# Moving the B multiply of the last state group from VectorE to GpSimd in a selective scan

## The chip, the core and the metric

The kernel runs on one core of a Trainium2 chip. Its five engines work side by side, each through its own instruction queue in order: TensorE (PE in the profile; its weight loads are PEld), VectorE (DVE), ScalarE (ACT), GpSimd (POOL) and SyncE (SP), which here only issues DMAs. The metric is the device time of one execution in microseconds, as the median of repeated runs.

## The reference

Two layers of a Perceiver-like model are applied to `x` of shape (16, 64, 256) in float32. Layer 0 has cross attention to a context of 1601 rows, a selective scan (Mamba) and a spiking feed-forward network. Layer 1 has a windowed cross attention with rotary embedding, a self attention with a distance mask, and a mixture of 8 experts. The change is in the selective scan of layer 0, which works on 512 channels and 16 states:

```python
def _selective_scan(u, delta, a, b, c):
    deltaA = jnp.exp(jnp.einsum('bld,dn->bldn', delta, a))
    deltaBu = jnp.einsum('bld,bln,bld->bldn', delta, b, u)

    def step(h, inp):
        dA_t, dBu_t, c_t = inp
        h = dA_t * h + dBu_t
        y = jnp.einsum('bdn,bn->bd', h, c_t)
        return (h, y)
    ...
    _, ys = lax.scan(step, h0, xs)
```

For each channel and state this is an elementwise product (delta·u times B), a linear recurrence along the 64 tokens of a batch row, a second product (with C), and a sum over the 16 states.

## The kernel before

The 1024 tokens are 8 tiles of 128. For the scan they are gathered in five groups of 1, 2, 2, 2 and 1 tiles (`GROUPS`), so a group has T = 128 or 256 token columns. `l0_ssm_prelude` computes for a group the projections, the convolution, delta and delta·u, and writes delta, delta·u, B and C to DRAM scratch. `l0_ssm_state` reads them back, laid out for the scan: the 128 partitions hold 4 states times 32 channels, and a tile of 4·T columns holds four such blocks of 32 channels. So one pass of the loops below handles one block of 128 channels (`c`, 4 of them) and one group of 4 states (`m`, 4 of them), and there are 5 × 4 × 4 = 80 passes. In each pass:

- ScalarE computes the decays exp(delta·a) with four activations (line 898) into one of two buffers `decay0`, `decay1` (`NDEC = 2`), used in turn;
- VectorE multiplies `rep["du"]` (delta·u) by B into a tile `hs` (line 906). There are two `hs` buffers (`HSB = 2`), so a pass can only start its multiply when the pass two before it has been consumed by TensorE;
- VectorE runs the recurrence in place over `hs` with one scan instruction (line 908);
- VectorE multiplies `hs` by C in place (line 909);
- TensorE adds up the states with four matmuls against `fold` into the PSUM tile `y_ps` (line 912).

B and C come in the tiles `bc0` (state groups 0 and 1) and `bc1` (2 and 3), broadcast over the four blocks of 32 channels. After the four state groups of a channel block, VectorE multiplies `y_ps` by the gate into `yg` (line 917). The tiles `rep_delta` and `rep_du` have two buffers each (`REPB = 2`) and are loaded by DMAs that SP issues (line 882).

GpSimd does smaller elementwise work elsewhere, among it: the softplus sum `spv` of the prelude (line 843, which is followed by the DMA to `d_delta`), the bias `xnb` of the first softmax (lines 605 to 607), the additions of bias rows to `x` (lines 543, 734, 1087, 1202), the rotary products `ku` and `kT` (line 1071) and the head-masked keys `ke` (line 1127) of the second cross attention.

The order of all this is not written out by hand. The program is built in a `TileContext` with `schedule_with_timeline_sim=True`: a list scheduler replays the instructions against a cost table (`scheduler_costs`) and chooses, by priority, what each engine issues next. The priorities are shifted by the table `AT`, with one number for each tile of cross attention (`C`), each group's prelude (`P`) and state part (`S`), each stage of the later layers (`D`) and the setup (`W`). So a change in the cost or the engine of one instruction, or in `AT`, can move any instruction on any queue. `Stream.new` gives out the working tiles of the later layers, with `BBUFS = 3` buffers for the larger ones.

Of the kernel before, what the change touches and what calls it, by code (L numbers as in the profile page):

```python
# [20 lines left out]
P = 128  # L21
B, L, D = 16, 64, 256
# [43 lines left out]
ABUFS, BBUFS, EBUFS = 6, 3, 4  # L66
# [17 lines left out]
WA = (0, 1)  # L84
GLAST = 0
SAFT = 1
AT = {'C': [-2654, 4379, 8514, -4563, 12435, 8604, 5776, 4319], 'P': [2517, -15292, 2786, -8356, -3704], 'S': [-11856, -1695, 3457, 4667, 7019], 'D': [634, 2469, 3629, 3736, 1255, 2078, 12241, 1395, 3496, 7769, 6287, -759, -2896, 7604, 9413, 8837, 2220, -6795, 6561, -231, 6259, 13545, -16171, 16810, 10814, 6655, 15499, 7678, 3528, 7791, 7607, 15099], 'W': [22194, 1512]}
LH = 1
PRI_D = [0] * 8
MOEB = {7:('bank0','bank1')}  # L90
# [8 lines left out]
PB = 8  # L99
PADX, PADR, PADC, SPLD, SPLM = 1, 1, 1, 1, 1  # L100
VPV = 0
ST1 = 1
SILU2 = 1
LNX, LNV, VBA, DSK = 1, ('c', 'p'), 1, 1
# [33 lines left out]
ABUFS = 6  # L138
BBUFS = 3
# [77 lines left out]
def kernel(ctx: ExitStack, tc: tile.TileContext, a: dict, out: bass.AP):  # L217
    nc = tc.nc
    A, V, G = nc.scalar, nc.vector, nc.gpsimd
# [41 lines left out]
    def sized(pool, tag, k, T, bufs=1, most=None):  # L261

        t = pool.tile([P, k * (most or GT)], F32, tag=tag, name=tag, bufs=bufs)
        return t[:, 0 : k * T].rearrange("p (k t) -> p k t", k=k)
# [90 lines left out]
    def at(kind, k):  # L355
        c = tc.cur_priority
        v = AT[kind][k]
        with tc.high_priority(0 if v is None else c - v):
# [4 lines left out]
    def after(k):  # L363
        return nullcontext() if k is None or k not in pe else tc.issue_after(pe[k].ins)

    def layernorm(new, bank, stp, x, nt):

        h = new("h", [P, nt, D])
        hT = new("hT", [P, KC, nt * P])
        mv = stp.tile([P, nt, 2], F32, tag="mv", name="mv")  # L370
        for j in range(nt):
# [50 lines left out]
    def mm_tok(ps, srcT, w, j):  # L422

        nk = w.shape[1]
        for kc in range(nk):
            nc.tensor.matmul(  # L426
                ps, srcT[:, kc, j * P : (j + 1) * P], w[:, kc, :],
                start=(kc == 0), stop=(kc == nk - 1),
            )
# [284 lines left out]
    def l0_ssm_prelude(w, pp, late, banks, g):  # L714
# [96 lines left out]
        for hf in range(2):  # L811
# [30 lines left out]
            V.copy_predicated(lg, mk, du)  # L842
            (V if VPV else G).tensor_add(vp, vp, lg)
            V.tensor_mul(du, vp, ug[:, 2 * hf : 2 * hf + 2, :])
# [17 lines left out]
    def l0_ssm_state(w, pp, s, g):  # L862
        i0, nt = GROUPS[g]
        T, nb = nt * P, 2 * nt
        x = xs[g]
        bc = []
        for q in range(2):
            t = sized(pp, f"bc{q}", 4, T)
            src = s["bc"][q * DST : (q + 1) * DST, :].rearrange("(k n) t -> n k t", n=SN)
            for n in range(SN):  # L870
                nc.sync.dma_start(
                    out=t[n * SD : (n + 1) * SD, :, :], in_=src[n].partition_broadcast(SD)
                )
            bc.append(t)
        yg = sized(pp, "yg", NE, T)
        for c in range(NE):
            rep = {}
            for k in ("delta", "du"):
                t = sized(pp, "rep_" + k, 4, T, bufs=REPB)
                src = s[k][c * P : (c + 1) * P, :].rearrange("(k d) t -> d k t", d=SD)  # L880
                for n in range(SN):
                    nc.sync.dma_start(out=t[n * SD : (n + 1) * SD, :, :], in_=src)
                rep[k] = t
            y_ps = psS.tile([P, T], F32, tag="y", name="y_ps")
            if DSK and SPLD:
                for k in range(4):
                    r = slice(k * SD, (k + 1) * SD)
                    nc.tensor.matmul(
                        y_ps[r, :], w["Dd"][:, c, r], s["ug"][:, c, :], start=True, stop=False
                    )  # L890
            elif DSK:
                nc.tensor.matmul(y_ps, w["Dd"][:, c, :], s["ug"][:, c, :], start=True, stop=False)
            for m in range(NG):
                da = w["decay"][turns[0] % NDEC][:, 0 : 4 * T]
                turns[0] += 1
                dav = da.rearrange("p (b l) -> p b l", l=L)
                for k in range(4):
                    A.activation(  # L898
                        dav[:, k * nb : (k + 1) * nb, 1:],
                        rep["delta"][:, k, :].rearrange("p (b l) -> p b l", l=L)[:, :, 1:],  # L900
                        AF.Exp,
                        scale=w["am"][:, c * 4 + k, m : m + 1],
                    )
                hs = sized(pp, "hs", 4, T, bufs=HSB)
                shp = [P, 4, T]
                V.tensor_mul(hs, rep["du"], bc[m // 2][:, m % 2, :].unsqueeze(1).to_broadcast(shp))  # L906
                hf = hs.rearrange("p k t -> p (k t)")
                V.tensor_tensor_scan(hf, da, hf, 0.0, ALU.mult, ALU.add)  # L908
                V.tensor_mul(hs, hs, bc[m // 2][:, 2 + m % 2, :].unsqueeze(1).to_broadcast(shp))  # L909
                with tc.high_priority(10**6):  # L910
                    for k in range(4):
                        nc.tensor.matmul(  # L912
                            y_ps[k * SD : (k + 1) * SD, :], fold, hs[:, k, :],
                            start=(m == 0 and not DSK), stop=(m == NG - 1),
                        )
            if DSK:
                V.tensor_mul(yg[:, c, :], y_ps, s["ug"][:, NE + c, :])
                continue
            V.scalar_tensor_tensor(
                yg[:, c, :], s["ug"][:, c, :], w["D"][:, c : c + 1], y_ps, ALU.mult, ALU.add  # L920
            )
            G.tensor_mul(yg[:, c, :], yg[:, c, :], s["ug"][:, NE + c, :])
        ps = psS.tile([P, nt, D], F32, tag="y", name="so_ps")
        for j in range(nt):
            mm_tok(ps[:, j, :], yg, w["out_w"], j)
        V.tensor_add(x, x, ps)
# [4 lines left out]
    class Stream:  # L931
# [9 lines left out]
        def new(self, name, shape):  # L941
            big = math.prod(shape[1:]) > D
            return self.pool.tile(
                shape, F32, tag=f"{'b' if big else 'a'}{self.k}", name=name,
                bufs=BBUFS if big else ABUFS,
            )

        def hidden(self):
# [498 lines left out]
    with tc.tile_pool(name="c0", bufs=1, side="right") as wp, tc.tile_pool(  # L1447
# [44 lines left out]
        for g, (i0, nt) in enumerate(GROUPS):  # L1492
            for i in range(i0, i0 + nt):
                hv, hs = HC.get(i, (None, None))
# [26 lines left out]
            if g < STATES:  # L1521
                with at("S", g):
                    l0_ssm_state(ws, sp, scratch[g], g)
# [105 lines left out]
    for i in range(NTI):  # L1629
        if i == RES:  # L1630
            tags = [("rep_delta", REPB), ("rep_du", REPB), ("hs", HSB), ("bc0", 1), ("bc1", 1)]
            tags = [t for t in tags for _ in range(t[1])]
            for e in range(NX):
                tag, bufs = tags[e]
                t = sized(sp, tag, 4, GT, bufs=bufs).rearrange("p (k c) n -> p k c n", k=2)
                for k in range(2):
                    nc.sync.dma_start(
                        out=t[:, k],
                        in_=a[f"L1_ffn_w{k + 1}"][e].rearrange("(c p) n -> p c n", p=P),
                    )  # L1640
                experts[e] = [t[:, 0], t[:, 1]]
        if TILE_STREAM[i] == NSTREAM:
            streams.append(LateStream(sp, NSTREAM, [(psS, t, 1) for t in BANK4]))
            vb, pb = (t[:, 0:n] for t, n in zip(ws["decay"], (2 * D, P)))
            for t in (vb, pb):
                G.memset(t, 0.0)
            if PADR or PADC:
                t = ws["decay"][1][:, P : P + PW]
                G.memset(t, 0.0)
                G.memset(t[:, 2:3], 1.0)  # L1650
                pads.append(t.unsqueeze(1))
            wx["vb"].append(vb.rearrange("p (b j h d) -> p b j h d", b=2, h=2, d=DH))
            wa["pb"].append(pb.unsqueeze(1))
        later(i)
        for g in range(STATES, len(GROUPS)):
            if i == AFTER[g]:
                with at("S", g), tc.issue_after(done[HOLD[g]]) if g in HOLD else nullcontext():
                    l0_ssm_state(ws, sp, scratch[g], g)
# [109 lines left out]
```

## Time and profile before

| quantity | value |
|---|---|
| median of 3 runs | 739.54 us (738.85 to 741.94) |
| profiled execution | 737.56 us |
| its span, first to last instruction | 735.7 us |
| PE busy | 631.6 us (86%) |
| DVE busy | 535.5 us (73%) |
| ACT busy | 453.2 us (62%) |
| POOL busy | 199.2 us (27%) |
| mean granted TensorE clock | 0.925 |

The profiled execution takes 1.9 us more than its span and lies 2.0 us under the median of the runs. Busy shares are averages over stages with different limits. The scan passes run from 87 us (first multiply, line 906) to about 565 us (last product with `fold`, line 912); the groups follow each other with passes of 128x512 for the first group until about 155 us, passes of 128x1024 for the three middle groups from about 158 to 488 us, and passes of 128x512 for the last group after that. Before lies the start of the first cross attention, behind it the rest of the later layers.

### The profile page before, as it was taken

To read this page: it belongs to the slowest core of one execution; us is meant where nothing else is said; L and a number is where in the kernel's file an instruction comes from. 1 tells how busy PE (TensorE), PEld (TensorE's weight loads), DVE (VectorE), ACT (ScalarE), POOL (GpSimd) and SP (SyncE) were. 2 spreads that over 40 slices of the span, in tenths; PEclk is the share of its full clock that TensorE was granted. 3 is DMA by queue.
4 is the path that set the end of the run, shared out by engine and by line. 5 is a ranking of instruction groups with operands and counts; after the bars stand their busy time and mean duration, and the time that the engine had idled before them with its cause. 6 is when DMAs were issued, how large, how long until landed. Compare 5 with 4: busy or idle time off the path is not lost.

```text
span 735.7 us, 12927 instructions
## 1 busy us (share of the span) xinstructions
PE 631.6 (86%) x4508; PEld 446.4 (61%) x4508; DVE 535.5 (73%) x937; ACT 453.2 (62%) x1442; POOL 199.2 (27%) x300
## 2 busy tenths in 40 slices
PE   9989888879997699864878695779889999999997
PEld 7555455535443487631536473357678787789986
DVE  3424578889999889999999899999776334444432
ACT  3446557845686458954987674478475657755422
POOL 3110020110003238033132966611053421133000
PEclk9999999989999679986889998599999999999999
DMA  8999699799834941122043021025457422000000
GB/s 302 333 367 356 185 324 289 257 270 353 256 120 122 318 132 30 37 67 71 1 128 97 2 58 30 11 62 140 143 169 244 122 58 73 9 1 8 8 15 7
DMA packets 85382, 102.55 MB, mean 139 GB/s; under 512 B 11515, under 2 KB 67763, under 8 KB 85190
## 3 DMA queue, kind: packets, MB, share of 16 engines
q1 hardware_dynamic: 85318, 101.74, 44.9%
q8 instruction: 35, 0.57, 0.3%
q14 instruction: 29, 0.24, 0.1%
HBM read 96.33 MB, written 5.37 MB: 138 GB/s over the span
## 4 chain that ended last, share of the span: by engine, by line
PE 47%; DVE 23%; ACT 11%; DMA 8%; POOL 5%; issue 5%; SPq 2%; DVEq 0%; POOLq 0%; ACTq 0%
PE he_ps L416 8%; PE eo_ps L426 7%; DVE hs L908 6%; DVE hs L906 5%; DVE hs L909 4%; PE s_ps L587 4%; PE o_ps L632 4%; ACT decay L898 3%; DMA w<-in_L_ffn_w 2%; PE fc_ps L416 2%; PE in_ps L416 2%; PE s_ps L1132 1%; PE pj_ps L426 1%; PE qk_ps L416 1%; DMA Wv<-in_L_attn_Wv 1%
## 5 line engine op out<-in xcount | busy, mean ns | idle before, releaser
L908 DVE TENSOR_TENSOR_SCAN hs<-decay,hs 128x1024 f32<-128x1024 f32 (+1 forms) x80 | 156.6, 1962 | 1.0 <-ACT decay L898 0.4
L898 ACT ACTIVATE decay<-rep_delta,ssm 128x252 f32<-128x252 f32 (+1 forms) x320 | 121.9, 455 | 50.7 <-DVE hs L908 36.7
L906 DVE TENSOR_TENSOR hs<-rep_du,bc 128x1024 f32<-128x1024 f32 (+1 forms) x80 | 86.9, 1091 | 19.3 <-PE y_ps L912 10.0
L909 DVE TENSOR_TENSOR hs<-hs,bc 128x1024 f32<-128x1024 f32 (+1 forms) x80 | 87.1, 1094 | 0.0
L1429 DVE SCALAR_TENSOR_TENSOR x<-eo_ps,pad,x 128x256 f32<-128x256 f32 x56 | 26.8, 479 | 46.1 <-PE eo_ps L426 45.5
L912 PE MATMUL y_ps<-hs,fold 128*32 128x256 f32 (+1 forms) x640 | 47.7, 383 | 14.5 <-DVE hs L909 14.2
L1418 ACT ACTIVATE he<-he_ps,late 128x128 f32<-128x128 f32 x112 | 35.1, 367 | 39.1 <-PE he_ps L416 39.0
L632 PE MATMUL o_ps<-cn,prT 128*64 128x256 f32 x384 | 52.5, 397 | 2.4 <-ACT prT L629 2.4
L587 PE MATMUL s_ps<-cT,qkT 128*64 128x512 f32 (+1 forms) x256 | 54.2, 509 | 0.2
L1127 POOL TENSOR_TENSOR ke<-kT,hmask 128x512 f32<-128x512 f32 x28 | 41.2, 1491 | 42.1 <-PE s_ps L1132 41.5
L632 PEld LDWEIGHTS o_ps<-cn,prT 128*64 128x64 f32 x384 | 28.1, 141 | 21.0 <-issue 5.9
L416 PE MATMUL in_ps<-hT,L_attn_in_proj_wT 128*128 128x256 f32 (+1 forms) x160 | 35.1, 371 | 4.5 <-ACT ug L760 3.8
L1139 ACT ACTIVATE sm<-s_ps,wmx 128x64 f32<-128x64 f32 x112 | 33.4, 322 | 3.5 <-DVE wmx L1136 3.4
L912 PEld LDWEIGHTS y_ps<-hs,fold 128*32 128x32 f32 x640 | 14.3, 113 | 34.4 <-DVE hs L909 19.8
L416 PEld LDWEIGHTS in_ps<-hT,L_attn_in_proj_wT 128*128 128x128 f32 x160 | 27.6, 210 | 12.5 <-ACT ug L760 5.5
L407 PE MATMUL pt_ps<-ident,h 128*128 128x128 f32 x88 | 20.4, 324 | 16.4 <-ACT h L395 13.6
L416 PE MATMUL he_ps<-hT,w 128*128 128x128 f32 x192 | 27.9, 291 | 7.5 <-DMA w<-in_L_ffn_w 7.1
L416 PE MATMUL fc_ps<-hT,L_ffn_W_fcT 128*128 128x128 f32 x224 | 32.3, 292 | 2.1 <-ACT f L998 1.6
L416 PEld LDWEIGHTS fc_ps<-hT,L_ffn_W_fcT 128*128 128x128 f32 x224 | 29.4, 202 | 7.2 <-ACT f L998 3.3
L765 DVE SCALAR_TENSOR_TENSOR ug<-xpad,ssm,ug 128x256 f32<-128x256 f32 (+1 forms) x60 | 26.4, 461 | 8.9 <-ACT ug L760 8.6
L605 POOL TENSOR_TENSOR xnb<-xmx,qb 128x1 f32<-128x1 f32 x8 | 2.7, 339 | 108.4 <-DVE xmx L594 91.9
L587 PEld LDWEIGHTS s_ps<-cT,qkT 128*64 128x64 f32 x256 | 17.5, 136 | 23.7 <-issue 20.0
(396 smaller groups left out, 1484.8 us busy)
## 6 DMA issues: line engine op xcount, KB each, us to landing
cn<-in_ctx SPq DMA_DIRECT2D x48, 512.0 KB, 5.4
cT<-in_ctxT SPq DMA_DIRECT2D x42, 512.0 KB, 8.2
w<-in_L_ffn_w SPq DMA_DIRECT2D x48, 256.0 KB, 2.7
rep_delta<-d_delta SPq DMA_DIRECT2D x48, 128.0 KB, 2.7
rep_du<-d_du SPq DMA_DIRECT2D x48, 128.0 KB, 3.1
bc<-d_bc SPq DMA_DIRECT2D x24, 128.0 KB, 3.6
rep_delta<-d_delta SPq DMA_DIRECT2D x32, 64.0 KB, 2.2
rep_du<-d_du SPq DMA_DIRECT2D x32, 64.0 KB, 2.1
```

What stands on the lines that cost most here:

```text
L416: last = nc.tensor.matmul(ps, w[:, kc, oc * P : (oc + 1) * P], src[:, kc, :], start=(kc == 0), stop=(kc == nk - 1),)
L426: nc.tensor.matmul(ps, srcT[:, kc, j * P : (j + 1) * P], w[:, kc, :], start=(kc == 0), stop=(kc == nk - 1),)
L587: nc.tensor.matmul(s_ps[r * L : (r + 1) * L, :n], q["qkT"][:, kc, r * L : (r + 1) * L], cT[r][:, kc, :], start=(kc == 0), stop=(kc == KC - 1),
L632: q["last"] = nc.tensor.matmul(q["o"][r * L : (r + 1) * L, :], prT[:n, j % 4, r * L : (r + 1) * L], cn[r, j], start=(j == 0), stop=(j == NKB),
L898: A.activation(dav[:, k * nb : (k + 1) * nb, 1:], rep["delta"][:, k, :].rearrange("p (b l) -> p b l", l=L)[:, :, 1:], AF.Exp, scale=w["am" ...
L906: V.tensor_mul(hs, rep["du"], bc[m // 2][:, m % 2, :].unsqueeze(1).to_broadcast(shp))
L908: V.tensor_tensor_scan(hf, da, hf, 0.0, ALU.mult, ALU.add)
L909: V.tensor_mul(hs, hs, bc[m // 2][:, 2 + m % 2, :].unsqueeze(1).to_broadcast(shp))
L912: nc.tensor.matmul(y_ps[k * SD : (k + 1) * SD, :], fold, hs[:, k, :], start=(m == 0 and not DSK), stop=(m == NG - 1),)
L1127: G.tensor_mul(ke, kT[:, c, tok].unsqueeze(1).to_broadcast([P, HPC, L]), hmask.unsqueeze(2).to_broadcast([P, HPC, L]),)
L1139: A.activation(sm[:, k, :], s_ps[:, k, :], AF.Exp, bias=nmx[:, k : k + 1], accum_out=su[i][:, c * HPC + k : c * HPC + k + 1],)
L1418: A.activation(he[:, oc, :], ps[:, oc, :], AF.Relu, bias=w["b1"][:, e * KC + oc : e * KC + oc + 1],)
```

## The change

For the last state group (`m == 3`) of every channel block, and for all five token groups, the multiply by B is issued to GpSimd in place of VectorE. The switch is a table `PM` from token group to pairs (state group, which multiply); the second multiply can be switched in the same way but no entry does so. A name `SHORT` could shorten a stream's buffers; it is empty, so nothing changes there. The table `AT` has new numbers throughout.

```diff
-AT = {'C': [-2654, 4379, 8514, -4563, 12435, 8604, 5776, 4319], 'P': [2517, -15292, 2786, -8356, -3704], 'S': [-11856, -1695, 3457, 4667, 7019], 'D': [634, 2469, ...], 'W': [22194, 1512]}
+AT = {'C': [-6091, 4373, 9420, -4172, 12134, 6772, 6015, 5883], 'P': [1045, -22019, 3863, -10472, -4579], 'S': [-20080, -1481, 3644, 6320, 7606], 'D': [699, 3387, ...], 'W': [23447, -4680]}
...
+SHORT = ()
+PM = {g: ((3, 0),) for g in range(5)}
...
-                V.tensor_mul(hs, rep["du"], bc[m // 2][:, m % 2, :].unsqueeze(1).to_broadcast(shp))
+                (G if (m, 0) in PM.get(g, ()) else V).tensor_mul(
+                    hs, rep["du"], bc[m // 2][:, m % 2, :].unsqueeze(1).to_broadcast(shp)
+                )
                 hf = hs.rearrange("p k t -> p (k t)")
                 V.tensor_tensor_scan(hf, da, hf, 0.0, ALU.mult, ALU.add)
-                V.tensor_mul(hs, hs, bc[m // 2][:, 2 + m % 2, :].unsqueeze(1).to_broadcast(shp))
+                (G if (m, 1) in PM.get(g, ()) else V).tensor_mul(
+                    hs, hs, bc[m // 2][:, 2 + m % 2, :].unsqueeze(1).to_broadcast(shp)
+                )
...
-                bufs=BBUFS if big else ABUFS,
+                bufs=BBUFS - (self.k in SHORT) if big else ABUFS,
```

So 20 multiplies change their engine, 12 of 128x1024 elements and 8 of 128x512. In the order in which the two programs are built, VectorE has 20 instructions fewer and GpSimd 20 more; on the other engines the instructions are the same and stand in a somewhat different order.

More of the change, by code (lines that the diff above doesn't have):

```diff
@@ L86 @@
 SAFT = 1
-AT = {'C': [-2654, 4379, 8514, -4563, 12435, 8604, 5776, 4319], 'P': [2517, -15292, 2786, -8356, -3704], 'S': [-11856, -1695, 3457, 4667, 7019], 'D': [634, 2469, 3629, 3736, 1255, 2078, 12241, 1395, 3496, 7769, 6287, -759, -2896, 7604, 9413, 8837, 2220, -6795, 6561, -231, 6259, 13545, -16171, 16810, 10814, 6655, 15499, 7678, 3528, 7791, 7607, 15099], 'W': [22194, 1512]}
+AT = {'C': [-6091, 4373, 9420, -4172, 12134, 6772, 6015, 5883], 'P': [1045, -22019, 3863, -10472, -4579], 'S': [-20080, -1481, 3644, 6320, 7606], 'D': [699, 3387, 5747, 3268, 1810, 2473, 14139, 1370, 3464, 7908, 4834, 1211, -4408, 8955, 8776, 12666, 2862, -6570, 6663, 390, 6477, 11509, -19814, 15316, 10812, 10825, 15642, 6273, 4889, 7190, 7666, 14068], 'W': [23447, -4680]}
 LH = 1
```

## The prediction

> **What bounds the kernel now.** I read the table of stretches first (busy time of each engine in chosen stretches), because busy shares over the whole span mix stages with different limits. Columns: PE, PEld, DVE, ACT and POOL busy microseconds, granted clock, DMA share, GB/s.
>
> ```profile
> 85.00:165.00 80.00, 64.36 (x493) 38.38 (x492) 65.77 (x111) 54.45 (x139) 10.91 (x14) 0.94 0.91 272
> 165.00:490.00 325.00, 255.49 (x1719) 161.87 (x1718) 310.90 (x407) 216.12 (x646) 123.07 (x124) 0.86 0.36 107
> ...
> 500.00:565.00 65.00, 59.25 (x528) 48.21 (x526) 49.91 (x90) 40.36 (x148) 12.86 (x20) 0.95 0.58 170
> 565.00:735.70 170.70, 163.85 (x1199) 140.08 (x1199) 69.07 (x215) 93.28 (x369) 36.12 (x84) 0.99 0.14 41
> ```
>
> From 165 to 490 us, where the three groups of two tiles are scanned, DVE is busy 310.90 of 325 us (96%) and PE 79%: DVE sets the pace there. Before (first group) DVE is at 82%, after 500 us PE at 91% and then 96%. So a microsecond of DVE time counts nearly in full in the middle stretch, partly at its edges. The second view is the groups of instructions by line and shape (busy us, mean ns of one, idle before them).
>
> ```profile
> L908 DVE TENSOR_TENSOR_SCAN hs<-decay,hs 128x1024 f32<-128x1024 f32 x48 | 115.7, 2411 | 0.4
> L906 DVE TENSOR_TENSOR hs<-rep_du,bc 128x1024 f32<-128x1024 f32 x48 | 64.9, 1354 | 7.9 <-DMA rep_du<-d_du 5.6 <-PE y_ps L912 2.3
> ...
> L906 DVE TENSOR_TENSOR hs<-rep_du,bc 128x512 f32<-128x512 f32 x32 | 22.0, 696 | 11.4 <-PE y_ps L912 7.7 <-DMA rep_du<-d_du 3.2 <-DMA cT<-in_ctxT 0.5
> ```
> ```profile
> L843 POOL TENSOR_TENSOR spv<-spv,hT 128x512 f32<-128x512 f32 x6 | 9.6, 1605 | 52.2 <-DVE hT L842 33.8 <-ACT spe L826 9.8 <-ACT decay L898 8.6
> ...
> L1127 POOL TENSOR_TENSOR ug<-ug,hmask 128x512 f32<-128x512 f32 x4 | 4.1, 1042 | 0.3 <-PE s_ps L1132 0.3
> ...
> L1071 POOL TENSOR_TENSOR ug<-ug,late 128x256 f32<-128x256 f32 x2 | 1.3, 639 | 0.0
> ```
>
> The reader should see two things. The mean of L906 at 128x1024 is 1354 ns, but most of its instructions take 1.21 us; and POOL's L843 has a mean of 1605 ns, while its shortest takes 1264. Something lengthens both. The third view, the timeline, shows what (start us, us):
>
> ```profile
> 170.88 1.27 POOL L734 TENSOR_TENSOR x<-x,L_attn_out_proj_b 128x512 f32<-128x512 f32 x1 [15.19 <-DVE h L385]
> ```
> ```profile
> 170.95 2.28 DVE L906 TENSOR_TENSOR hs<-rep_du,bc 128x1024 f32<-128x1024 f32 x1
> 173.27 2.29 DVE L908 TENSOR_TENSOR_SCAN hs<-decay,hs 128x1024 f32<-128x1024 f32 x1
> ```
> ```profile
> 328.00 5.05 POOL L734 TENSOR_TENSOR x<-x,L_attn_out_proj_b 128x256 f32<-128x256 f32 x1 [1.60 <-DVE h L385]
> ```
>
> POOL's addition runs from 170.88 to 172.15. The DVE multiply that starts at 170.95 takes 2.28 us: the 1.20 us until POOL is done, and then 1.08, its usual time. The other way round, POOL's 128x256 addition at 328.00, which takes 0.73 us undisturbed, takes 5.05 while DVE issues a multiply, a scan and other instructions with two SBUF inputs back to back. So DVE and POOL do not overlap in such work; they take turns.
>
> **What is removed.** Twelve DVE multiplies of 128x1024 and eight of 128x512. Start to start they cost 1.135 and 0.60 us (medians over the undisturbed ones of L906; the recorded 1.21 and 0.68 overlap the next instruction by 0.08). Sum: 12 × 1.135 + 8 × 0.60 = 18.4 us of DVE.
>
> **What is added.** The same multiplies on POOL, which the trace does not show there. The nearest rows are its multiplies with one operand broadcast over an outer dimension: L1071 (0.64 us for 256 columns) and L1127 (1.04 for 512), both from a stretch where DVE leaves POOL alone. The line through them gives 1.85 us for 1024. The additions without a broadcast give 0.72 and 1.265, so 2.35 for 1024; that is the upper bound. POOL's queue gets 12 × 1.85 + 8 × 1.04 = 30.5 us (upper bound 12 × 2.35 + 8 × 1.265 = 38.3), beside 123 of 325 us in the middle stretch: it does not become the bound by its amount.
>
> **What DVE pays for it.** If the two took no notice of each other, DVE would be 18.4 us shorter. The trace says otherwise. The eight 128x512 additions of L843 and L734 that fall between 138 and 330 us lengthened the DVE instructions under them by 1.09, 0.44, 1.10, 1.04, 1.00, 0.99, 0.79 and 0.78 us, in mean 0.90 of their own 1.265: all but 0.36 us. L1127's twenty in the same kind of stretch cost DVE 0.59 of 1.04: all but 0.45. I take 0.40 us off each: the time in which POOL starts up, or DVE happens to run something that reads PSUM or one tile. Then a moved multiply of 1024 costs DVE 1.45 and saves 1.135, net +0.32 us; one of 512 costs 0.64 and saves 0.60, net +0.04. Sum: 12 × 0.32 + 8 × 0.04 = +4.1 us. The bounds: every POOL microsecond stalls DVE, 30.5 − 18.4 = +12.1; or the average of the whole stretch from 160 to 500 us holds, where all DVE lengthenings together are 30.5 us for 63.4 us of undisturbed POOL reading work, a share of 0.48, which gives 14.6 − 18.4 = −3.8. That average counts many 128x1 instructions that hardly read, so I stay with the rows of the large ones.
>
> The Trainium skill has a rule that speaks against this change (SBUF — State Buffer, "Who interferes with whom"): a DVE instruction with two SBUF inputs and a GpSimd instruction that reads SBUF shut each other out, and whichever began first keeps the shared port for its whole length. Taken to the letter, with DVE always second, the sum would be the +12.1 already given; the rows above say somewhat less.
>
> **The new wait.** The scan of `m == 3` (L908) now waits for POOL. What is queued behind it on DVE is its own multiply by C, the next block's multiplies and whatever the later layers have there, and ACT waits too, since the decay buffers come free with the scans (ACT idled 36.7 us on L908 before). In the built order DVE has the scan and the C multiply of `m == 2` ahead of it, 2.20 + 1.135 us, and other work: the stretch has 310.9 − 48 × 4.47 = 96 us of it, 2.0 us a pass; 5.3 us together, counted from the C multiply of `m == 1`, which frees the `hs` buffer. POOL needs the four L912 matmuls (4 × 0.44 = 1.8), its 1.85, and the wait for its turn: all POOL instructions together took 0.85 times longer than undisturbed there, so about 1.6. That is 5.2: just covered, so zero; without that cover it costs up to 1.6 us a block, 12 × 1.6 = 19.
>
> **What else moves.** On POOL the moved multiply stands ahead of `xnb` (L605, ACT's first softmax waits for it), `spv` (L843, then SP's `d_delta` DMA; SP's queue waited 21.5 us for it before) and the `ke` pairs (PE). POOL stood idle 91.9 us before L605 and 41.5 before L1127, waiting for others, so 2 to 3 us of delay lie beside DVE's work: zero. `rep_du`'s loads on SP (L882, which waited 16.9 us for L906) now wait for POOL's read; with two buffers they have a whole block of time: zero. The new `AT` table moves instructions on every queue, but ahead of the last scan DVE has the same other work to within 1% and the same 80 passes in the same order: zero, with bounds of ±3 us from the largest single DVE waits in the stretch (2.7 us, L906 for a DMA). `SHORT` is empty: zero.
>
> **Sum.** The profiled execution is 735.7 of span + 1.9 around it = 737.6 us; +4.1 gives 741.7. Its time lies 2.0 under the median of the runs, 739.54, so the forecast is 743.6 us.
>
> **The rivals.** One half percent, 3.7 us, is about what a measurement here can tell from no change.
>
> *Gain by overlap (faster).* POOL's multiplies fall where DVE reads PSUM or waits, as in the stretch from 400 to 500 us, where the share of POOL time that DVE paid was 0.31: 9.5 − 18.4 = −8.9; with the share 0.48, −3.8. So 730.6 to 735.7. It decides if the share is under 0.60 − 3.7/30.5 = 0.48. For it speaks that DVE no longer holds its queue at L906 for `y_ps` (7.7 us in the 512 rows). Against it: scans and `hs` multiplies of 128x1024, all with two SBUF inputs, are 115.7 + 64.9 + 63.5 = 244 of DVE's 311 us there.
>
> *Break-even.* The share is between 0.48 and 0.72 and nothing waits: within 3.7 us of 739.5.
>
> *Slower by the turn-taking.* My forecast, share 0.72 and more, up to 1: +4 to +12, 743.6 to 751.6.
>
> *Slower by the wait at the scan.* POOL gets its turn late, as at 328.00, in half the blocks: 6 × 1.6 = 10 on top of break-even, 749; it decides once POOL's waits exceed the cover of 5.3 us.
>
> **How the numbers follow.** Turn-taking 0.36, wait at the scan 0.11, break-even 0.18, overlap 0.35. So faster 0.35, same 0.18, slower 0.47. The range goes from the lower overlap case, 730.6, to just above the full turn-taking, 753. The forecast's own range is 740 to 752.
>
> **What would show it.** Right: in the changed kernel L908 and the C multiplies that start just after a POOL multiply are longer by about 1.4 us, POOL's multiplies take 1.85 us undisturbed and more in the mean, and the middle stretch is longer with DVE still above 95% busy. Wrong: DVE lengthenings that grow by less than 15 us in total, or scans of `m == 3` with long idle time before them released by POOL, or a stretch other than 165 to 490 that changes.

## The result: 2.8% slower, and the profile after

The changed kernel takes 759.34 us (median of 4 runs, 757.79 to 759.61); the kernel before takes 739.19 us on the same chip (4 runs). The ratio is 1.0277, 95% interval 1.0218 to 1.0337. The forecast was 743.6 with a range of 730 to 753, so the sign of the likeliest case was right and the size was not: +20.2 us where +4.1 was forecast. The profiled spans differ by as much, 756.1 against 735.7. Of the runs of the variants below, two executions that were slow as a whole are left out of the medians: one of `a_mid` (829.91 us, at a granted clock of 0.72 where its others have 0.91 to 0.92) and one of `a_memset_q` (760.41 us).

First the page's busy times, then the table of stretches of the changed kernel, cut where its groups begin and end. Columns: PE, PEld, DVE, ACT and POOL busy microseconds with instruction counts, granted clock, DMA share, GB/s. Code lines have moved in the changed kernel: the multiply by B is L908, the scan L912, the multiply by C L913, the fold L918.

```profile
PE 635.5 (84%) x4508; PEld 450.5 (60%) x4508; DVE 538.9 (71%) x917; ACT 450.6 (60%) x1442; POOL 248.2 (33%) x320
```
```profile
85.00:165.00 80.00, 64.34 (x483) 37.43 (x480) 65.15 (x106) 52.86 (x135) 18.10 (x18) 0.94 0.90 275
165.00:525.00 360.00, 277.67 (x1860) 181.65 (x1859) 324.97 (x420) 229.31 (x713) 157.78 (x138) 0.84 0.34 99
525.00:590.00 65.00, 56.58 (x513) 44.85 (x511) 54.24 (x101) 39.62 (x142) 25.61 (x38) 0.97 0.60 175
590.00:756.10 166.10, 158.51 (x1149) 136.21 (x1141) 63.74 (x199) 89.06 (x350) 31.67 (x69) 1.00 0.13 39
```

DVE has 20 instructions fewer (917 against 937) and is busy 3.4 us longer. The middle stretch has become longer, 360 us against 325, and DVE is busy 90% of it against 96%: it has both more busy time and more idle time. The groups by line and shape show where the busy time comes from (busy us, mean ns of one, idle before), first DVE's, then POOL's:

```profile
L913 DVE TENSOR_TENSOR hs<-hs,bc 128x1024 f32<-128x1024 f32 x48 | 66.2, 1381 | 0.1
L908 DVE TENSOR_TENSOR hs<-rep_du,bc 128x1024 f32<-128x1024 f32 x36 | 49.6, 1380 | 10.3 <-PE y_ps L918 4.5 <-DMA rep_du<-d_du 3.2 <-DMA bc<-d_bc 2.6
```
```profile
L908 POOL TENSOR_TENSOR hs<-rep_du,bc 128x1024 f32<-128x1024 f32 x12 | 32.9, 2738 | 52.9 <-PE y_ps L918 23.0 <-DMA rep_delta<-d_delta 16.5 <-DMA cn<-in_ctx 13.4
...
L908 POOL TENSOR_TENSOR hs<-rep_du,bc 128x512 f32<-128x512 f32 x8 | 12.0, 1505 | 43.3 <-PE y_ps L918 43.1
```

DVE's 36 multiplies by B at 1024 columns take 1380 ns in the mean, where the undisturbed ones take 1.21 us; POOL's take 2738, where its undisturbed ones take 2.35 us. Each lengthens the other. The timeline shows single moved multiplies with the DVE instruction that meets them (start us, us):

```profile
223.30 2.86 POOL L908 TENSOR_TENSOR hs<-rep_du,bc 128x1024 f32<-128x1024 f32 x1 [17.12 <-PE y_ps L918]
224.53 1.91 DVE L833 TENSOR_SCALAR spm<-spe 128x512 uint8<-128x512 f32 x1 [0.29 <-ACT spe L828]
...
346.58 2.47 POOL L908 TENSOR_TENSOR hs<-rep_du,bc 128x1024 f32<-128x1024 f32 x1 [16.50 <-DMA rep_delta<-d_delta]
346.77 4.43 DVE L912 TENSOR_TENSOR_SCAN hs<-decay,hs 128x1024 f32<-128x1024 f32 x1
...
375.94 2.35 POOL L908 TENSOR_TENSOR hs<-rep_du,bc 128x1024 f32<-128x1024 f32 x1 [3.02 <-PE y_ps L918]
376.10 2.50 DVE L844 COPY_PREDICATED hT<-spm,h 128x256 f32<-128x256 uint8 x1
```

The scan at 346.77 takes 4.43 us where 2.2 is usual; the small instruction at 376.10, whose shortest takes 0.46, takes 2.50 and ends just after POOL does. These two began inside a POOL multiply and stood until it was done. It isn't only instructions with two input tiles that stand: the comparison L833 (`tensor_scalar`, one input tile, 128x512) that starts at 224.53 inside the multiply of 223.30 takes 1.91 us, where three others of its shape take 0.39 to 0.40. The undisturbed multiply takes POOL 2.35 us at 1024 columns and 1.27 at 512.

To see the whole of it I split DVE's time from its first instruction to the last scan into three parts, from the trace: gaps between instructions (idle); what each instruction takes over the tenth percentile of its own operation, tile and shape (lengthening); and the rest (plain). The same split is used for the experiments. The last four columns come from one profiled execution each; those of `b_shrunk` and `a_shrunk` lie 3 to 4 us under their medians, so differences of that size in the time of the last scan say nothing.

| kernel | median us (before, same chip) | idle | lengthening | plain | last scan at |
|---|---|---|---|---|---|
| before | 739.19 | 95.9 | 41.4 | 421.5 | 560.5 |
| after | 759.34 (739.19) | 112.9 | 63.1 | 406.9 | 584.6 |
| `b_shrunk` | 736.85 (738.24) | 108.2 | 40.5 | 406.2 | 556.5 |
| `a_shrunk` | 736.97 (738.24) | 111.7 | 39.4 | 407.0 | 559.7 |
| `b_plus` | 750.73 (739.78) | 94.5 | 41.5 | 437.8 | 575.4 |
| `b_all` | 713.92 (739.78) | 137.2 | 37.2 | 359.6 | 535.5 |
| `q_zero` | 743.63 (738.70) | 129.0 | 33.5 | 414.5 | 578.7 |
| `q_fill` | 746.39 (738.70) | 129.8 | 34.3 | 415.0 | 580.9 |
| `q_mul` | 762.92 (738.70) | 119.8 | 58.7 | 414.8 | 595.2 |
| `a_edge` | 737.78 (738.00) | 107.5 | 45.3 | 406.6 | 561.3 |
| `a_mid` | 759.40 (738.00) | 114.6 | 59.7 | 406.7 | 583.0 |

From before to after, plain time falls by 14.6 (the 18.4 removed, less other work that now lies ahead of the last scan, about 2.5 us of it by the shortest times of these instructions), lengthening rises by 21.7, and idle time rises by 17.0: the last scan is 24.1 later, and the tail behind it 3.7 shorter. The added idle time is hardly a wait for POOL: with POOL's multiplies cut (`a_shrunk`) it is 111.7, nearly the same.

### The profile page after: what moved, and what is told of

It is laid out like the page before. It is cut to its first block, busy times and chain, and to the rows that moved or that the text cites. A ratio compares the mean times of both kernels' runs of the same rounds, so it can differ in the third digit from the quotient of the medians.

```text
span 756.1 us, 12976 instructions
## 1 busy us (share of the span) xinstructions
PE 635.5 (84%) x4508; PEld 450.5 (60%) x4508; DVE 538.9 (71%) x917; ACT 450.6 (60%) x1442; POOL 248.2 (33%) x320
## 4 chain that ended last, share of the span: by engine, by line
PE 29%; DVE 6%; DMA 5%; POOL 4%; issue 3%; ACT 2%; SPq 1%; POOLq 0%; DVEq 0%
PE he_ps L418 7%; PE eo_ps L428 7%; DMA w<-in_L_ffn_w 4%; DVE hs L912 2%; PE s_ps L1138 2%; PE pj_ps L428 2%; PE fc_ps L418 1%; PE o_ps L1166 1%; DVE hs L913 1%; POOL hs L908 1%; PE pt_ps L409 1%; DVE hs L908 1%; PE f_ps L1353 1%; POOL ke L1133 1%; PE p_ps L1155 1%
## 5 line engine op out<-in xcount | busy, mean ns | idle before, releaser
L912 DVE TENSOR_TENSOR_SCAN hs<-decay,hs 128x1024 f32<-128x1024 f32 (+1 forms) x80 | 157.4, 1973 | 5.7 <-POOL hs L908 5.4
L913 DVE TENSOR_TENSOR hs<-hs,bc 128x1024 f32<-128x1024 f32 (+1 forms) x80 | 90.0, 1130 | 0.1
L908 DVE TENSOR_TENSOR hs<-rep_du,bc 128x1024 f32<-128x1024 f32 (+1 forms) x60 | 66.2, 1107 | 17.4 <-PE y_ps L918 8.3
L908 POOL TENSOR_TENSOR hs<-rep_du,bc 128x1024 f32<-128x1024 f32 (+1 forms) x20 | 44.9, 2245 | 96.2 <-PE y_ps L918 66.0
L918 PE MATMUL y_ps<-hs,fold 128*32 128x256 f32 (+1 forms) x640 | 49.0, 388 | 30.3 <-DVE hs L913 30.3
L918 PEld LDWEIGHTS y_ps<-hs,fold 128*32 128x32 f32 x640 | 14.3, 114 | 50.0 <-DVE hs L913 38.2
L428 PE MATMUL pj_ps<-L_ffn_W_projT,f 128*128 128x256 f32 x112 | 32.1, 439 | 1.6 <-ACT f L1005 0.9
```

The source lines that it names most:

```text
L428: nc.tensor.matmul(ps, srcT[:, kc, j * P : (j + 1) * P], w[:, kc, :], start=(kc == 0), stop=(kc == nk - 1),)
L908: (G if (m, 0) in PM.get(g, ()) else V).tensor_mul(hs, rep["du"], bc[m // 2][:, m % 2, :].unsqueeze(1).to_broadcast(shp))
L913: (G if (m, 1) in PM.get(g, ()) else V).tensor_mul(hs, hs, bc[m // 2][:, 2 + m % 2, :].unsqueeze(1).to_broadcast(shp))
L918: nc.tensor.matmul(y_ps[k * SD : (k + 1) * SD, :], fold, hs[:, k, :], start=(m == 0 and not DSK), stop=(m == NG - 1),)
```

## The experiments

In most of them the order of the instructions on every queue was held fixed, by telling the scheduler the old cost of an instruction that had been cut; so a difference is that of the instruction and not of a new plan. The code shown is cut down: the lines that tell the scheduler the old cost are left out, and names such as `da_part_k` stand for longer slices. Names with `b_` have the order of the kernel before, names with `a_` that of the changed one.

### 1. What are the saving and the cost worth, each alone?

`b_shrunk` takes the 20 DVE multiplies away from the kernel before, without giving them to POOL. `a_shrunk` takes them away from POOL in the changed kernel.

```diff
-V.tensor_mul(hs, rep["du"], bc[m // 2][:, m % 2, :].unsqueeze(1).to_broadcast(shp))   # m == 3
+V.tensor_mul(hs[:, 0, 0:nt], rep["du"][:, 0, 0:nt], bc[m // 2][:, m % 2, 0:nt])       # G in a_shrunk
-V.tensor_tensor_scan(hf, da, hf, 0.0, ALU.mult, ALU.add)
+V.tensor_tensor_scan(hf, da, bc[1].rearrange("p k t -> p (k t)"), 0.0, ALU.mult, ALU.add)
```

> The kernel before with the same 20 multiplies cut to one or two columns on VectorE, order kept (the product of the last state group is left out of the result). It measures what 18.4 us of DVE time are worth in the old order. If DVE is the bound of the scan stretch: 739 - 16 to 18, that is 721 to 723 us. If other engines take over as the bound: 728 to 735 us.

> The changed kernel with the GpSimd multiply cut down to one or two of its 512 or 1024 columns (the scan of that pass reads B and C values in place of the product, so this part of the result is left out); the scheduler is told the old duration, so the order on every queue stays that of the changed kernel. Theory 1 (GpSimd's reads stall DVE, and late products cause the waits): the 21.7 us of added DVE lengthening and the 17 us of added idle time both go, 720 to 727 us. Theory 2 (the new order is the worse one): the lengthening goes and the idle time stays, about 738 us. If neither DVE lengthening nor waits matter: 755 us or more.

Measured: `b_shrunk` 736.85 us, ratio 0.9987 (0.9956 to 1.0018); `a_shrunk` 736.97, ratio 0.9984 (0.9953 to 1.0015). Both are level with the kernel before and with each other. So the saved DVE time is worth nothing that can be told from zero here (at most about 3 us, by the interval), the new order with its new `AT` table costs nothing by itself, and the whole loss of about 22 us is what POOL's full-length multiplies do.

In `b_shrunk` DVE's plain time is 15.3 us shorter and its idle time 12.3 us longer. Its waits between 88 and 562 us (us in total, times, longest) show that the time went into several, here the kernel before and then `b_shrunk`:

```profile
DVE hs L906 <- PE y_ps L912: 10.0, 8, 2.2
...
DVE hs L906 <- DMA rep_du<-d_du: 5.6, 2, 2.9
```
```profile
DVE hs L917 <- DMA rep_du<-d_du: 9.6, 2, 5.4
DVE hs L917 <- PE y_ps L926: 9.4, 12, 2.2
...
DVE hs L917 <- DMA rep_delta<-d_delta: 3.3, 1, 3.3
DVE total L1034 <- ACT y L1033: 2.9, 3, 1.3
```

### 2. Does DVE's time count in the other direction?

`b_plus` makes the same 20 multiplies slower on DVE, with POOL untouched; `b_all` cuts all 80.

```diff
-V.tensor_mul(hs, rep["du"], bc[...]...)                                   # m == 3, b_plus
+V.tensor_tensor_scan(hs_flat, rep_du_flat, bc_flat, 0.0, ALU.mult, ALU.mult)
```

> The kernel before, its order kept, with the twenty DVE multiplies by B of the last state group made slower: each is a scan over the same two tiles (2.3 us in place of 1.2 at 1024 columns), so DVE has about 12 x 1.13 + 8 x 0.6 = 18 us more and POOL nothing new. Its output differs. Theory 'kink' (DVE's time counts in full upwards, though the same 18 us taken away bring nothing): 754 to 758. Theory 'slack' (DVE time counts neither way in this plan, and POOL's part has another cause): 738 to 745.

> The kernel before, its order kept, with all eighty DVE multiplies by B cut to one or two columns (the scans read the B rows): four times the 15 us that were taken away before. Theory 'other chains close behind' (loads, ACT's decays and PE's folds set the pace as soon as DVE is a little shorter): 725 to 736. Theory 'a bounded slack' (the first 15 us go into waits, and what is taken away beyond that counts): 738 - 46 = 692. If DVE counted in full: 677.

Measured: `b_plus` 750.73, ratio 1.0151 (1.0099 to 1.0203); `b_all` 713.92, ratio 0.9661 (0.9603 to 0.9720). In their profiles DVE's plain time is 16.3 longer and 61.9 shorter. So 16 us more cost 11, 15 us less bring 1, and 62 us less bring 26: the price of a microsecond of DVE is about 0.7 upwards, and downwards 0.1 for the first fifteen and 0.5 for the next 47. Both times lie between the forecasts of their two theories, so neither theory holds as stated: there is a kink, and beneath it time taken away is worth little at first and more later.

### 3. Reading, or holding POOL's queue?

`b_lock` was meant to run POOL reading work beside the scans with nobody waiting for it.

```diff
 scan = V.tensor_tensor_scan(hf, da, hf, 0.0, ALU.mult, ALU.add)
+with tc.issue_after(scan.ins):                # m == 2
+    for _ in range(2 * nt): G.tensor_mul(junk, ident_broadcast, ones_broadcast)
```

> The kernel before, order kept, DVE keeps all its multiplies; GpSimd gets extra multiplies of 128x256 that nobody waits for, four in each of 12 passes and two in each of 8 (64 of them, 0.7 us each alone, 45 us in all), started behind the scan of the third state group. Theory 1: DVE pays about half to three quarters of it, 739 + 22 to 34 = 761 to 773 us. Without a shared turn: 739 to 741 us.

Measured: 771.67 us, ratio 1.0460 (1.0397 to 1.0523), but it does not test what it was meant to. Its inputs are constants, and all 64 extra multiplies ran between 3 and 60 us, ahead of the first scan:

```profile
L918 POOL TENSOR_TENSOR junk<-ident,ones 128x256 bf16<-128x256 f32 x64 | 46.5, 726 | 4.9
```

DVE's lengthening stayed at 41.6 us, and the first scan came at 124.5 in place of 88.2. What it shows is that POOL's queue at the start is on the path: 46.5 us of work nobody needs cost 33.

`a_nowait` and `a_memset_q` tie the extra work to a place by making it read the pass's decays (`da`), and let the scan wait only for a two-column multiply.

```diff
 G.tensor_mul(hs[:, 0, 0:nt], rep["du"][:, 0, 0:nt], bc[...][:, m % 2, 0:nt])
+for k in range(nt + 1): G.tensor_mul(junk, rep["du"][:, k, :], da_part_k)              # a_nowait
+G.tensor_mul(junk[:, 0, 0:nt], rep["du"][:, 0, 0:nt], da[:, 0:nt])                     # a_memset_q
+for _ in range((5, 9)[nt - 1]): G.memset(junk, 1.0)                                    # a_memset_q
```

> The changed kernel with its order on every queue, but the scan of the last state group waits only for a POOL multiply of one or two columns (and reads the B rows in place of the product); behind that multiply POOL runs two (one-tile group) or three (two-tile groups) multiplies of 128x256 of rep_du and the decays into a scratch tile that nobody reads: 12 x 3 x 0.73 + 8 x 2 x 0.73 = 38 us of POOL reading work, as much as the moved multiplies. Theory 'port' (the loss is DVE standing still while POOL reads, whoever waits for the result): DVE's lengthenings come back to about 60 us and the time is 755 to 760. Theory 'wait' (the loss is the scan waiting for POOL's product): 737 to 742 as with the shrunk multiply, in spite of the lengthenings.

> The same kernel and order, but behind the short multiply POOL fills the scratch tile with constants (five or nine memsets of 128x256): its queue is held for about as long, and nothing is read from SBUF. Theory 'port': DVE's lengthenings stay at about 40 us and the time at 736 to 740. Theory 'POOL's queue' (what stands behind the moved multiply on POOL, such as the softmax's and the keys' small instructions, is late and that is the loss): 750 to 760.

Measured: `a_nowait` 755.94, ratio 1.0225 (1.0174 to 1.0275), with 55.9 us of lengthenings, as if the loss needed nobody who waits for POOL's product. But `a_memset_q`, which reads nothing in its long part, takes 753.12, ratio 1.0168 (1.0094 to 1.0243), with lengthenings of only 36.4. That looked like the queue theory. The waits of POOL show that the edits brought a wait of their own, which the changed kernel does not have, here in `a_nowait` and then in `a_memset_q`:

```profile
POOL junk L924 <- ACT decay L906: 95.2, 12, 19.1
```
```profile
POOL junk L919 <- ACT decay L906: 87.4, 10, 17.8
```

The first extra instruction holds POOL's queue until ACT has made the decays, 95.2 and 87.4 us in total, and what stands behind it can start late. The pair can't separate the two causes, so three further kernels were made with one common order: two memsets and a multiply into the scan's own tile, with the waits of the changed kernel and no other. They differ only in which of them is whole.

```diff
+for _ in range(2): G.memset(hs if FILL else hs[:, 0, 0:nt], 0.5)
-G.tensor_mul(hs, ...)
+G.tensor_mul(hs if MUL else hs[:, 0, 0:nt], ...)
```

> Control of three kernels with one common order on every queue (close to the changed kernel's): for the last state group POOL runs two memsets and one multiply, all of one or two columns, into the tile that the scan overwrites, so the scan waits for POOL as in the changed kernel, but POOL is done at once; the scan reads the B rows. Expected by every theory: 736 to 743, about the kernel before, DVE's lengthenings about 40 us.

> The same order, but the two memsets fill the whole tile: POOL is held for 2 x 1.03 + 0.2 = 2.3 us at 1024 columns (as long as the moved multiply), the scan waits for that, and nothing is read from SBUF. Theory 'port' (only the reading costs, through DVE): within 4 us of the control. Theory 'queue and wait' (the scan, and what stands behind on POOL, wait for POOL's 2.3 us): 10 to 20 us above the control, with DVE's lengthenings unchanged at about 40 us and more idle time of DVE.

> The same order, the two memsets small, and the multiply whole, as in the changed kernel (2.35 us at 1024 columns, 1.27 at 512, two SBUF inputs). Port theory: about 20 us above the control (756 to 764), of which 20 to 24 are DVE lengthenings. Queue and wait: as much above the control as the filling memsets are, 10 to 20 us.

Measured: `q_zero` 743.63, ratio 1.0058 (1.0024 to 1.0091), so the common order by itself costs some 4 us and the three are compared with one another; `q_fill` 746.39, 1.0115 (1.0050 to 1.0180); `q_mul` 762.92, 1.0333 (1.0277 to 1.0388). POOL's groups in `q_fill` and then `q_mul`:

```profile
L915 POOL MEMSET hs<- 128x1024 f32 x24 | 22.8, 951 | 54.6 <-PE y_ps L933 54.0
...
L915 POOL MEMSET hs<- 128x512 f32 x16 | 8.4, 525 | 39.9 <-PE y_ps L933 39.5
```
```profile
L917 POOL TENSOR_TENSOR hs<-rep_du,bc 128x1024 f32<-128x1024 f32 x12 | 37.8, 3148 | 1.3 <-POOL hs L915 0.2 <-DMA d_delta<-spv 0.2
...
L917 POOL TENSOR_TENSOR hs<-rep_du,bc 128x512 f32<-128x512 f32 x8 | 11.2, 1401 | 0.7
```

Two memsets of 0.95 us hold POOL for nearly as long as one multiply of 2.35, and the scan waits for them too. In place the multiply took 3.15 in the mean, since it also waits for DVE: all instructions of these two lines together hold POOL for 42.9 us in `q_fill` and 52.9 in `q_mul`. The memsets cost 2.8 us over the control, with hardly any lengthening (34.3 against 33.5). The multiply costs 19.3, with 25.2 us of lengthening. So about 16.5 of 19.3 us come with POOL's reading beside DVE; the queue and the wait at the scan are the other 2.8, no more than the intervals allow. That POOL's own delay by DVE makes the scan wait is not the rest of it: in `q_mul` DVE's scans wait for POOL's product 2.4 us in all.

```profile
DVE hs L927 <- POOL hs L917: 2.4, 2, 1.7
```

### 4. Where does a microsecond of lengthening count?

`a_edge` and `a_mid` split the moved multiplies on the changed kernel's order: whole only in the first and last group, or whole only in the three groups between.

```diff
+WHOLE = (0, 4)      # a_edge;  (1, 2, 3) in a_mid
-G.tensor_mul(hs[:, 0, 0:nt], ...)
+G.tensor_mul(hs, ...) if g in WHOLE else G.tensor_mul(hs[:, 0, 0:nt], ...)
```

> The changed kernel's order on every queue; POOL's multiply is whole only in the first and the last group (eight of 128x512), in the three groups between it is cut to two columns (and the scan of that pass reads the B rows everywhere). With all twenty cut the time was 737, with all whole 759. Lengthenings of about 8 x 0.8 = 6 us come back. If a microsecond of DVE counts only where DVE is never idle: 737 to 740. If it counts everywhere: 742 to 745.

> The complement: POOL's multiply is whole only in the three middle groups (twelve of 128x1024), where DVE is busy 96% of the time; about 12 x 1.5 = 18 us of lengthenings. If the middle carries the loss: 754 to 760. If the edges carry a share by their number: 749 to 753.

Measured: `a_edge` 737.78, ratio 0.9999 (0.9971 to 1.0027); `a_mid` 759.40, ratio 1.0301 (1.0243 to 1.0360). Against `a_shrunk`, 5.9 us of lengthening in the outer groups cost 0.8 us (with an interval of about 3 us either way), and 20.3 us in the middle cost 22.4. The middle carries the loss, whole within the intervals.

### 5. What stands beside DVE when its time is cut?

Two crossings on the kernel before: PE's folds cut to two columns, or ACT's decays to one column of each sequence, each with and without the 20 cut multiplies.

```diff
-nc.tensor.matmul(y_ps[k * SD : (k + 1) * SD, :], fold, hs[:, k, :], ...)       # pe_pl, pe_dve
+nc.tensor.matmul(y_ps[k * SD : (k + 1) * SD, 0:2], fold, hs[:, k, 0:2], ...)
-A.activation(dav[:, k * nb : (k + 1) * nb, 1:], ...)                           # act_pl, act_dve
+A.activation(dav[:, k * nb : (k + 1) * nb, 1:2], ...)
```

> The kernel before with its order on every queue; the folding matmuls into y_ps (320 of them) are cut to two columns, so PE is lighter by most of their time and y_ps frees hs sooner. DVE's work is whole. If DVE sets the pace of the scans alone: 728 to 737. If PE stands level with it: 700 to 725.

> The same, and the twenty multiplies by B of the last state group are cut too (15 us of DVE). Theory 'PE stands behind DVE': 10 to 15 us faster than the run with the folds cut alone. Theory 'other chains': within 4 us of it, as without the cut folds (where the 15 us brought 1.4).

> The kernel before with its order; ACT's decays (320 activations) are cut to one column of each sequence block, so ACT is lighter by most of their time and decays come sooner; the scans' length is unchanged. DVE's work is whole. If DVE sets the pace alone: 728 to 737; if ACT stands level with it: 700 to 725.

> The same, and the twenty multiplies by B of the last state group are cut too. Theory 'ACT stands behind DVE': 10 to 15 us faster than the run with the decays cut alone. Theory 'other chains': within 4 us of it.

Measured: `pe_pl` 739.88 (ratio 1.0014, 0.9977 to 1.0051) and `pe_dve` 737.61 (1.0008, 0.9976 to 1.0041); `act_pl` 734.26 (0.9953, 0.9923 to 0.9983) and `act_dve` 732.85 (0.9930, 0.9896 to 0.9964). The cut multiplies bring 2.3 us beside lighter folds (0.4 by the ratios) and 1.4 beside lighter decays, about as they brought 1.4 without; none of these can be told from zero. So neither PE's folds nor ACT's decays alone stand behind DVE. The loads of `rep_du` and `rep_delta` and the work that prepares the next group are left; that they are it was not tried, and stays open.

### 6. The table of due times, and an attempt at a faster kernel

`pm_old_at` is the change with the old `AT` table; `b_vpv` is the kernel before with `VPV = 1`, which puts the softplus sums (line 843) on DVE, away from POOL.

> The change with the old table of priorities: only the multiplies move. Theory 1: the table does not matter, 754 to 764 us. Theory 2 in the form that the new table makes the order worse: 740 to 748 us.

> The kernel before with the softplus sums (the ten additions of spv) on DVE in place of POOL; the scheduler makes its own order, with the old table of due times. DVE gets about 6 x 0.6 + 4 x 0.33 = 5 us, and about 6 x 0.9 + 4 x 0.4 = 7 us of lengthenings go. Theory 'kink' (DVE time taken away brings nothing in this plan): 735 to 745, no gain. If DVE's lengthenings counted in full in both directions, with a shorter way to the loads of delta as well: 730 to 735.

Measured: `pm_old_at` 764.21, ratio 1.0359 (1.0313 to 1.0405): the new table is worth about 5 us within the change, at the edge of what the intervals tell apart, and nothing without the POOL work (`a_shrunk`). `b_vpv` 755.38, ratio 1.0236 (1.0184 to 1.0288): the lengthenings fell to 31.4 us, but DVE's plain time rose by 6.4 and the last scan is at 563.3, no earlier than before; another 18 us are lost behind it, where more work lies now (PE is busy 181.6 us after 565 us, against 163.9). The scheduler made this order with a table made for another program, so it is no fair test of that move. No version here that computes the whole result beats the kernel before.

## Why the prediction was wrong, point by point

**"A microsecond of DVE time counts nearly in full in the middle stretch" is the step that failed**, in its use for time that is taken away: `b_shrunk` lost 15.3 us of DVE time and gained 1.4. For time that is added it held (`a_mid`: 22.4 us for 20.3). The forecast subtracted the 18.4 us removed at full price. With zero in its place the same sum would have been 0 + 22.5 = +22.5, against +20.2 measured. The mistake was to read the price from DVE's busy share, 96%. The page before has a view that speaks against it, the chain that ended last, with the shares of the span by engine:

```profile
PE 47%; DVE 23%; ACT 11%; DMA 8%; POOL 5%; issue 5%; SPq 2%; DVEq 0%; POOLq 0%; ACTq 0%
```

Added up piece by piece between 165 and 490 us, the chain before has 144 us of DVE in 326, 56 of PE, 46 of ACT, 35 of POOL and 20 of DMA, the rest being issue and queues; of the 20 multiplies that were moved only nine are on it, 8.65 us. At one place it leaves DVE altogether (start us, us, what):

```profile
234.71 3.20 DVE hs L908
237.91 0.02 issue
237.94 1.69 ACT decay L898 x4
...
240.52 10.07 DMA Wv<-in_L_attn_Wv
...
251.43 4.28 DMA c<-in_c64T
```

From here to 310.02 the chain has no DVE instruction, while DVE is busy 65.9 of those 72 us. So an engine can be nearly full and not be what the end waits for. In `b_shrunk` DVE's share of this chain fell to 16%, in `a_shrunk` to 20%. The chain is no exact price either: it would have allowed 8.65 us for the saving, where 1.4 came.

Where the time went is seen in the middle groups, from the end of the 16th scan to the end of the 64th:

| kernel | stretch, us | length | DVE busy | DVE idle |
|---|---|---|---|---|
| before | 153.3 to 485.9 | 332.6 | 315.6 | 17.0 |
| `b_shrunk` | 153.6 to 486.3 | 332.7 | 301.9 | 30.8 |
| `b_plus` | 155.5 to 502.1 | 346.6 | 327.7 | 18.9 |
| `a_shrunk` | 153.6 to 484.2 | 330.6 | 301.1 | 29.5 |
| `a_mid` | 153.7 to 504.7 | 351.0 | 322.0 | 29.0 |
| after | 155.7 to 502.7 | 347.0 | 319.5 | 27.6 |

Time taken away turns into idle time of the same size, and the stretch stays as long. Time added makes the stretch longer by about as much, in `b_plus` and also in `a_mid`, where DVE has 29.5 us of idle time before the addition and 29.0 after it. So the gaps that the saving opens don't take up the lengthenings, and a total of idle time is no reserve. Why they don't, and what holds the stretch at 331 to 333 us when DVE's part is lighter, the runs do not show; section 5 rules out PE's folds and ACT's decays, each alone.

**What is added** was priced 1.85 and 1.04 us from the multiplies L1071 and L1127; it is 2.35 and 1.27, the upper bound from the additions. The two rows taken had a broadcast operand as the moved multiply has, but different shapes and strides, and that a broadcast makes POOL faster was never shown. POOL's undisturbed work is 38.3 us, not 30.5, and in place it took 44.9.

**What DVE pays** was put at 22.5 us and is 21.7, but by two errors that cancel, which is luck: the share is 0.57 of 38.3, not 0.74 of 30.5. The sign named in advance, some 1.4 us more for the instruction beside a POOL multiply, was too low too: 2.0 to 2.2 us beside most of those of 128x1024. The Trainium skill's rule (SBUF — State Buffer, "Who interferes with whom"), that a DVE instruction with two SBUF inputs and a GpSimd instruction that reads SBUF shut each other out, agrees with the overlaps shown here: the scan at 346.77 pays 2.2 of POOL's 2.47 us. In the sum the share is lower. Four of the 20 multiplies lengthened nothing: at 256.79 DVE ran nothing, at 412.06 a reduction of the PSUM tile `s_ps`, at 533.02 and 550.62 an addition with a PSUM input and small instructions. The other sixteen lengthened DVE by about 25 us, so lengthenings elsewhere must have fallen by some 4.

**The new wait** at the scan was put at zero, with up to 19 us if uncovered. DVE's waits in the changed kernel have it three times:

```profile
DVE hs L912 <- POOL hs L908: 5.4, 3, 2.6
```

`q_fill` prices this wait and the held queue together at 2.8 us, for a POOL that is held 42.9 us: near enough to zero, and the cover did hold in most passes.

**The rest.** The new plan at zero was right (`a_shrunk` and `b_shrunk` differ by 0.1 us). POOL's other work behind the moved multiply at zero was right for this change, but perhaps not safe: `a_memset_q`, with POOL's queue held by a new wait, lost some 13 us with no more lengthening than before. "Partly at the edges" can't be judged: there a lengthening of 5.9 us cost 0.8, with an interval of about 3 us. Of the four rivals none left the saving out, so none could reach 759; the highest, 751.6, took the full exclusion and still subtracted 18.4. The sign named in advance, "DVE still above 95% busy" in the middle, failed, at 90%: the time saved came back as idle time.

## What to carry to other kernels

Don't price time taken from a busy engine by its busy share. The share of the chain that ended last warns of it, but gave too much here too (8.65 us, where 1.4 came); only the run with the work cut and the order kept gave the price. Time added to DVE in its full stretch cost its whole length, even in a kernel where the saving had opened gaps. Moving two-input elementwise work from DVE to POOL made DVE pay more than it saved, 1.08 us for each 0.92 (21.7 and 18.4 over 20 multiplies), so even at equal prices it did not pay here. Test the saving and the cost separately, with the order of the queues held fixed, before believing their difference.

## What the runs showed of the hardware that was not expected

The moved POOL multiply, with an operand broadcast over an outer dimension, takes as long as a plain addition of that size where both were measured (1.27 us at 128x512, and 2.35 at 128x1024, on the line of the additions), though the multiplies L1071 and L1127, which also have broadcast operands, are shorter (0.64 us at 128x256, 1.04 at 128x512); what makes the difference stays open. POOL memsets of 0.95 us at 128x1024 left DVE's lengthenings where they were (34.3 against 33.5 us), so these POOL instructions, which only write, did not shut DVE out. And a DVE instruction that waits in this way is recorded as a longer instruction, not as a wait, so the loss appears in no list of waits: 0.46 us became 2.50 at 376.10.
